# An adaLN attention and expert kernel: the scores of pairs at the clamped distance, from the content product instead of blocks of relative terms

## The chip, the cores and the metric

The kernel runs on one core of one Trainium2 chip. The metric is the device time of one execution in microseconds (us), lower is better. TensorE is called PE, VectorE DVE, ScalarE ACT, GpSimd POOL, and SP is the engine that here only issues DMAs.

## The reference, cut to what matters

There are 16 batches of 512 positions and 256 features, 16 heads of 16. After a layer norm with modulation comes an attention with relative position embeddings in both directions, then a second norm and a mixture of 8 experts of which the best two are summed. All is in float32. The part that the change touches:

```python
scores = jnp.einsum('bhqd,bhkd->bhqk', q, k)
dist_idx = pos_l - pos_r + M - 1                 # M = 256, S = 512
pos_emb = dist_emb[dist_idx]                     # dist_emb has 511 rows
rel_q = jnp.einsum('bhld,lrd->bhlr', q, pos_emb)
rel_k = jnp.einsum('bhrd,lrd->bhlr', k, pos_emb)
scores = (scores + rel_q + rel_k) / sqrt(D)
probs = softmax(scores)
```

The index runs up to 511 + 255, beyond the last row, 510. An index past the end is clamped to 510. For the last query tile (positions 384 to 511) and the first key tile (positions 0 to 127) every index is at least 512, so all pairs there have one and the same embedding row e. With q, k and e the score before the scale is then q.k + q.e + k.e = (q + e).(k + e) - e.e.

## The kernel before, in words

The work is cut into three kinds of pieces.

The **prologue** (`prepare`, one call per batch) normalizes a batch, transposes it on PE, forms q, k and v and stores them to DRAM. `normalize(b + 1)` is called inside `prepare(b)`, so DVE normalizes a batch while PE works on the one before. Between the calls for the first batches stands the setup: small loads, the gates, and the tables `t_f` and `t_r` (the embedding rows as PE's moving operand), loaded by 16 DMAs on SP at L509 and L512. `stationary` then rewrites q and k as stationary operands in DRAM.

A **block of terms** (class `Rel`, 64 of them) holds rel_q + rel_k for 128 pairs of batch and head, 64 queries and 128 keys. Block n stands for a half s of the batches, a query tile lb, a key tile rb and a half lh of the query tile. `q_set` (L165, four times per block) multiplies q with a table into four PSUM banks, which ACT copies out (L175). `k_set` (L186, four times) does it for k, and DVE adds the four banks (L195). `store` writes the block to `rel_d` in DRAM (L203). The first 10 blocks (`LEAD`) are made in the prologue, the rest beside the units.

A **unit** (64 of them) is one query tile of 128 positions of one batch, all 16 heads, from the scores to the output. Unit u has s = u // 32, lb = u % 32 // 8, so units 24 to 31 and 56 to 63 have the last query tile, lb = 3. For each of four groups of four heads: `load_scores` fetches the terms from `rel_d` into `st` (L582); `content` multiplies q with k, masked so that head pairs share a row group, four matmuls of 32 rows by 512 columns (L644), and DVE adds the terms and takes the row maxima (L650); ACT takes the exponentials (L660); `turn` transposes (L669) and ACT or DVE evicts; `context` multiplies with v (L687), and ACT copies the unit's context out once (`cT`, L695). After that: `project` with a norm (its `rstd`, a power, on POOL, L101), `residual` (three POOL operations, L754 to L756), `norm2` (stats on DVE, `rstd` on POOL again at L101, then `xn` on DVE, L768), `modulate` (transposes `fpt` of xn on PE, L778), `route`, and the experts in four pairs (L830), whose results DVE and ACT take from PSUM (L841, L845) and POOL sums up (L851 to L855). `mask_q` forms the masked q for the next unit with two POOL operations (`qm`, L614).

The order on every engine is written out by hand: each unit has 16 slots, and a step is put in a slot by `at(slot, order, function, ...)`. Steps of one slot run in the order of the second number. Each engine takes its instructions in that order. The lines that matter here, z being the unit's first slot:

```python
at(q0 - 12, 0, load_scores, u, g)   # q0 = z + 4 * g
at(q0 - 4, 5, content, u, g)
at(z - 13, 0, load_k, u, 0)
at(z - 6, 0, load_k, u, 1)
at(z - 7, 0, mask_q, u)
z += 16
at(z + 8, 0, residual, u)
at(z + 10, 0, norm2, u)
at(z + 11, 6, modulate, u)
n = u + LEAD                        # block n beside unit u
```

So `mask_q` of the next unit stands on POOL between `residual` and `norm2` of the unit before. PSUM has seven banks in one pool (`bank`), handed out in turn to all of these steps, and one for the context.

Of the kernel before, what the change touches and what calls it, by code (L numbers as in the profile page):

```python
# [8 lines left out]
F32 = mybir.dt.float32  # L9
U32 = mybir.dt.uint32  # L10
AF = mybir.ActivationFunctionType
ALU = mybir.AluOpType
AX = mybir.AxisListType
# [3 lines left out]
P = 128  # L17
E = 256
S = 512
H = 16  # L20
D = 16
# [5 lines left out]
NP = 64  # L27
HB = 8
LQ = 64
RK = 128  # L30
# [4 lines left out]
def adaln_attention_moe_kernel(  # L35
# [34 lines left out]
    nc = tc.nc  # L70
    NB = x.shape[0]
    NL = S // P
    NE = E // P
# [6 lines left out]
    const = ctx.enter_context(tc.tile_pool(name="const", bufs=1))  # L80
# [6 lines left out]
    par = const.tile([P, 2], F32, name="par")  # L87
# [5 lines left out]
    t_f = const.tile([P, 2, 2 * S], F32, name="t_f")  # L93
    t_r = const.tile([P, 2, 2 * S], F32, name="t_r")

    wo_sb = const.tile([P, NE, E], F32, name="wo_sb")
    gates_d = dram.tile([NB, 3, E], F32, name="gates_d")

# [16 lines left out]
    rel_d = [dram.tile([P, P, S], F32, tag=f"rel_{n}", name=f"rel_d{n}") for n in range(8)]  # L115
# [6 lines left out]
    def bank(name):  # L122
        return ps.tile([P, S], F32, tag="g", name=name)


    class Rel:


        def __init__(self):
            self.qe = {}  # L130
            self.ke = {}
            self.two = [rblk.tile([P, LQ, RK], F32, name=f"r_{i}") for i in range(2)]

        @staticmethod
        def at(n):
            s, m = n // 32, n % 32
            return s, m // 8, m % 8 // 2, m % 2

        def wants(self, n):

            s, lb, rb, lh = self.at(n)
            w = []
            if rb == 0:
                w += [("q", s, lb * 2 + lh, g) for g in range(2)]
            if lh == 0:
                w += [("k", s, rb * 2 + g // 2, g % 2) for g in range(4)]
            return w
# [60 lines left out]
    rel = Rel()  # L208


    with ExitStack() as pro:
# [205 lines left out]
        with tc.tile_pool(name="setup", bufs=1) as su:  # L417
# [7 lines left out]
            for name, w in (("wq", wq), ("wk", wk), ("wv", wv)):  # L425
                nc.scalar.dma_start(
                    out=w_sb[name], in_=w.rearrange("(kc p) n -> p kc n", p=P)
# [33 lines left out]
            for k, kind in enumerate((0, 1, 3, 4)):  # L461
                for cc in range(NE):
                    col = kind * E + cc * P
                    for kc in range(NE):
                        nc.tensor.matmul(
                            pm[:, k, cc, :], wm[:, kc, col : col + P], scT[:, kc, :],
                            start=(kc == 0), stop=(kc == NE - 1),
# [10 lines left out]
            for k, kind in enumerate((2, 5)):  # L478
                for kc in range(NE):
                    nc.tensor.matmul(  # L480
                        pg[:, k, :], scT[:, kc, :], wm[:, kc, kind * E : (kind + 1) * E],
                        start=(kc == 0), stop=(kc == NE - 1),
# [23 lines left out]
            for t in range(4):  # L506
                for i in range(2):
                    rows = slice(32 * t + 16 * i, 32 * t + 16 * i + 16)
                    nc.sync.dma_start(  # L509
                        out=t_f[rows, i, i : 2 * S], in_=ext[:, 0 : 2 * S - i]  # L510
                    )
                    nc.sync.dma_start(  # L512
                        out=t_r[rows, i, i : 2 * S - 1], in_=rev[:, 0 : 2 * S - 1 - i]
                    )
            m8 = su.tile([P, 8], F32, name="m8")
            nc.gpsimd.memset(m8, 1.0)
            nc.gpsimd.affine_select(
                out=m8, in_=m8, compare_op=ALU.is_ge, fill=0.0,
# [3 lines left out]
                out=m8, in_=m8, compare_op=ALU.is_ge, fill=0.0,  # L522
# [7 lines left out]
        for cc in range(NE):  # L530
            for pa in range(2):
                for t in range(4):
                    row = cc * P + t * 32 + pa * D
                    nc.sync.dma_start(
                        out=wo_sb[pa * 64 + t * D : pa * 64 + (t + 1) * D, cc, :],
                        in_=wo[row : row + D, :],
# [16 lines left out]
    u1 = ctx.enter_context(tc.tile_pool(name="u1", bufs=1))  # L553
    u2 = ctx.enter_context(tc.tile_pool(name="u2", bufs=2))
# [16 lines left out]
    def place(u):  # L571
        s, lb, bb = u // 32, u % 32 // 8, u % 8
        return s, lb, bb, s * HB + bb

    units = {}

    def load_scores(u, g):

        s, lb, bb, b = place(u)
        h0 = bb * H + (g // 2) * 8 + g % 2  # L580
        st = sp.tile([P, 4, S], F32, tag="s", name=f"s_{u}_{g}")
        nc.sync.dma_start(  # L582
            out=st, in_=rel_d[s * 4 + lb][h0 : h0 + 7 : 2].rearrange("h l r -> l h r")
        )
        units[u]["s", g] = st

    def load_k(u, cc):
        s, lb, bb, b = place(u)
        kt = kp.tile([P, S], F32, tag="k", name=f"k_{u}_{cc}")
        nc.sync.dma_start(  # L590
            out=kt,
            in_=k_d[s][bb * H + cc * 8 : bb * H + cc * 8 + 8].rearrange("h d l -> (h d) l"),
        )
        units[u]["k", cc] = kt

    def load_q(u):
        s, lb, bb, b = place(u)
        lcols = slice(lb * P, (lb + 1) * P)
        qs = u1.tile([P, NE, P], F32, tag="qs", name=f"qs_{u}")
        for cc in range(NE):  # L600
            nc.sync.dma_start(
                out=qs[:, cc, :],
                in_=q_d[s][bb * H + cc * 8 : bb * H + cc * 8 + 8, :, lcols].rearrange(
                    "h d l -> (h d) l"
                ),
            )
        units[u]["qs"] = qs

    def mask_q(u):

        qs = units[u].pop("qs")
        qm = u2.tile([P, 2, NE, P], F32, tag="qm", name=f"qm_{u}")
        for pa in range(2):
            nc.gpsimd.tensor_scalar(qm[:, pa], qs, par[:, pa : pa + 1], None, ALU.mult)  # L614
        units[u]["q"] = qm

    def load_rest(u):
        s, lb, bb, b = place(u)
# [18 lines left out]
    def content(u, g):  # L637

        t_ = units[u]
        cc, pa = g // 2, g % 2  # L640
        bs = [bank(f"qk_{u}_{g}_{t}") for t in range(4)]
        for t in range(4):
            rows = slice(32 * t, 32 * t + 32)
            nc.tensor.matmul(  # L644
                bs[t], t_["q"][rows, pa, cc, :], t_["k", cc][rows, :], start=True, stop=True
            )
        mx = u3.tile([P, 4], F32, tag="mx", name=f"mx_{u}_{g}")
        st = t_["s", g]
        for t in range(4):
            nc.vector.tensor_tensor_reduce(  # L650
                st[:, t, :], bs[t], st[:, t, :], 0.25, -3.0e38, ALU.add, ALU.max,
                mx[:, t : t + 1],
            )
        nc.vector.tensor_scalar(mx, mx, -1.0, None, ALU.mult)  # L654
        t_["m", g] = mx
# [180 lines left out]
    def expert_sums(u, pr):  # L836

        t_ = units[u]
        py = t_.pop("py")
        e = 2 * pr  # L840
        nc.vector.scalar_tensor_tensor(  # L841
            t_["y"], py[:, 0:E], t_["mask"][:, e : e + 1], t_["y"], ALU.mult, ALU.add
        )
        ye = u2.tile([P, E], F32, tag=f"ye{pr > 0}", name=f"ye_{u}_{pr}")
        nc.scalar.activation(  # L845
            ye, py[:, E : 2 * E], AF.Identity, scale=t_["mask"][:, e + 1 : e + 2]
        )
        if pr == 0:
            t_["y2"] = ye
        else:  # L850
            nc.gpsimd.tensor_tensor(t_["y2"], t_["y2"], ye, ALU.add)  # L851
        if pr == NX // 2 - 1:
            nc.gpsimd.tensor_tensor(t_["y"], t_["y"], t_["y2"], ALU.add)
            nc.gpsimd.tensor_tensor(t_["y"], t_["y"], t_["gf"], ALU.mult)
            nc.gpsimd.tensor_tensor(t_["y"], t_["y"], t_["x2"], ALU.add)  # L855
# [12 lines left out]
    for u in range(NP):  # L868
        z = 16 * u
        for g in range(4):  # L870
            q0 = z + 4 * g
            at(q0 - 12, 0, load_scores, u, g)
            at(q0 - 4, 5, content, u, g)
            at(q0 - 2, 7, exps, u, g, (0, 1))
            at(q0 - 1, 7, exps, u, g, (2, 3))
            for t in range(4):
                at(q0 + t, 3, turn, u, g, t, t > 0)
            at(q0 + 5, 4, context, u, g)
        at(z - 16, 0, lambda u: units.setdefault(u, {}), u)
        at(z - 13, 0, load_k, u, 0)  # L880
        at(z - 6, 0, load_k, u, 1)
        at(z - 15, 0, load_q, u)
        at(z - 7, 0, mask_q, u)
        at(z - 9, 0, load_rest, u)
        at(z + 15, 0, load_tail, u)
        z += 16
        at(z + 3, 6, back, u)
        at(z + 5, 3.5, contextT, u)
        at(z + 7, 6, project, u)
# [3 lines that stand above are left out]
        at(z + 13, 7, route, u)  # L893
        at(z + 15, 7, mask_t, u)
        at(z + 16, 7, bias, u)
        for pr in range(4):
            at(z + 18 + 4 * pr, 6, experts, u, pr)
            at(z + 19 + 4 * pr, 1, expert_sums, u, pr)
        at(z + 35, 0, finish, u)

        z -= 16
        n = u + LEAD
        if n < NP:
            for g in range(4):
                at(z + 1 + 4 * g, 6, rel.q_set, n, g)
                at(z + 15 + 4 * g, 2, rel.k_set, n, g)
            for g in range(4):
                at(z + 28 + 2 * g, 0, rel.store, n, g)
        if n + 1 < NP:
            for w in rel.wants(n + 1):  # L910
                o = 8 + w[3] if w[0] == "q" else (16, 17, 21, 25)[w[2] % 2 * 2 + w[3]]
                at(z + o, 0, rel.load, w)
# [52 lines left out]
```

## Time and profile before

| | |
|---|---|
| median of 3 runs | 2974.68 us (2971.85 to 2978.81) |
| profiled execution | 2971.56 us, span 2969.8 us |
| granted PE clock, mean of the span | 0.971 |
| busy share PE / DVE / ACT / POOL | 95% / 67% / 65% / 21% |
| first and last context copy (`cT`) | 528.8 us, 2934.5 us |
| L165 and L186, the blocks' matmuls, busy | 467.1 and 321.2 us |
| L644, content matmuls, busy | 388.9 us |
| moved by DMA | 796.46 MB |

Up to some 520 us lies the prologue with the first ten blocks, then the units follow each other. The first 54 have a block beside them, the last ten have none. Busy time of an engine is the union of its instructions. In a timeline each row has the start, the length, the engine, the line, the operation, what is written from what is read, the shape, how many instructions were merged into the row, and in brackets how long the engine stood idle before it and what it had waited for. "SPq" is the issue of a DMA, not its transfer.

### The profile page before, as it was taken

To read this page: it belongs to the slowest core of one execution; us is meant where nothing else is said; L and a number is where in the kernel's file an instruction comes from. 1 tells how busy PE (TensorE), PEld (TensorE's weight loads), DVE (VectorE), ACT (ScalarE), POOL (GpSimd) and SP (SyncE) were. 2 spreads that over 40 slices of the span, in tenths; PEclk is the share of its full clock that TensorE was granted. 3 is DMA by queue.
4 is the path that set the end of the run, shared out by engine and by line. 5 is a ranking of instruction groups with operands and counts; after the bars stand their busy time and mean duration, and the time that the engine had idled before them with its cause. 6 is when DMAs were issued, how large, how long until landed. Compare 5 with 4: busy or idle time off the path is not lost.

```text
span 2969.8 us, 75984 instructions
## 1 busy us (share of the span) xinstructions
PE 2815.0 (95%) x30186; PEld 1845.8 (62%) x30186; DVE 1984.0 (67%) x5396; ACT 1933.7 (65%) x3682; POOL 629.8 (21%) x863
## 2 busy tenths in 40 slices
PE   8889864999999999999999999999999999999997
PEld 5556552666666666666666666666666666666564
DVE  5446542777777777777767777677777767776664
ACT  2344433777776777777677677777767777767774
POOL 1000000121222222122222212222222222222333
PEclk9889866999999999999999999999999999999999
DMA  6879997798988889988888998888898888898661
GB/s 191 302 260 319 298 302 259 229 290 268 287 269 271 280 283 293 280 272 281 272 271 277 287 281 274 268 283 277 281 295 268 286 273 272 272 280 279 211 232 54
DMA packets 855346, 796.46 MB, mean 268 GB/s; under 512 B 25545, under 2 KB 649409, under 8 KB 854737
## 3 DMA queue, kind: packets, MB, share of 16 engines
q1 hardware_dynamic: 854032, 790.03, 84.3%
q8 instruction: 240, 3.93, 0.5%
q10 hardware_dynamic: 960, 1.57, 0.2%
q14 instruction: 114, 0.93, 0.1%
HBM read 462.20 MB, written 328.25 MB: 266 GB/s over the span
## 4 chain that ended last, share of the span: by engine, by line
PE 79%; POOL 2%; DMA 1%; DVE 1%; SPq 1%; issue 1%; ACT 1%; POOLq 0%; ACTq 0%; DVEq 0%
PE pt L669 18%; PE fpy L830 14%; PE pq L165 13%; PE qk L644 12%; PE pc L687 8%; PE pk L186 8%; PE ph L735 2%; PE fpl L791 1%; PE pcl L702 1%; POOL qm L614 1%; DMA vu<-v_d 1%; PE fpt L778 1%; PE fpb L821 0%; PE pct L719 0%; POOL rstd L101 0%
## 5 line engine op out<-in xcount | busy, mean ns | idle before, releaser
L175 ACT COPY r<-pq 128x512 f32<-128x512 f32 x1024 | 525.4, 603 | 385.8 <-PE pq L165 368.9
L195 DVE TENSOR_TENSOR r<-pk,r 128x512 f32<-128x512 f32 x1024 | 635.0, 683 | 192.8 <-PE pk L186 187.3
L660 ACT ACTIVATE s<-s,mx 128x512 f32<-128x512 f32 x1024 | 691.6, 735 | 50.2 <-DVE mx L654 47.2
L650 DVE CUSTOM_DVE_ANT_0 s<-qk,s 128x512 f32<-128x512 f32 x1024 | 644.0, 685 | 39.2 <-PE qk L644 36.7
L669 PE MATMUL pt<-ident,s 128*128 128x128 f32 x4096 | 652.0, 283 | 10.7 <-ACT s L660 10.3
L669 PEld LDWEIGHTS pt<-ident,s 128*128 128x128 f32 x4096 | 451.0, 142 | 289.3 <-issue 77.7
L672 ACT COPY pT<-pt 128x512 f32<-128x512 f32 x768 | 459.5, 598 | 252.1 <-PE pt L669 250.4
L851 POOL TENSOR_TENSOR ye<-ye,ye 128x256 f32<-128x256 f32 x192 | 140.6, 732 | 1633.0 <-ACT ye L845 1627.5
L830 PE MATMUL fpy<-we_sb,fhT 128*128 128x512 f32 x1024 | 483.4, 595 | 0.0
L165 PE MATMUL pq<-t_r,qe 32*128 32x256 f32 x4096 | 467.1, 417 | 4.0 <-DMA qe<-eq_d 2.9
L644 PE MATMUL qk<-k,qm 32*128 32x512 f32 x2048 | 388.9, 644 | 28.0 <-POOL qm L614 28.0
L186 PEld LDWEIGHTS pk<-t_f,ke 32*128 32x128 f32 x8192 | 268.8, 190 | 189.1 <-ACT pT L672 157.7
L841 DVE SCALAR_TENSOR_TENSOR fy<-fpy,fmask,fy 128x256 f32<-128x256 f32 x256 | 123.8, 483 | 384.6 <-PE fpy L830 375.6
L165 PEld LDWEIGHTS pq<-t_r,qe 32*128 32x128 f32 x4096 | 283.3, 186 | 143.1 <-DVE mx L650 67.8
L186 PE MATMUL pk<-t_f,ke 32*128 32x128 f32 x8192 | 321.2, 288 | 7.2 <-DVE r L195 3.4
L687 PE MATMUL pc<-pT,vu 128*32 128x128 f32 x8192 | 278.2, 277 | 0.0
L830 PEld LDWEIGHTS fpy<-we_sb,fhT 128*128 128x128 f32 x1024 | 175.4, 191 | 124.9 <-issue 124.9
L687 PEld LDWEIGHTS pc<-pT,vu 128*32 128x32 f32 x8192 | 209.2, 110 | 43.5 <-issue 42.9
L644 PEld LDWEIGHTS qk<-k,qm 32*128 32x128 f32 x2048 | 141.5, 183 | 104.6 <-DVE r L195 47.3
L674 DVE COPY pT<-pt 128x512 f32<-128x512 f32 x256 | 174.5, 682 | 24.9 <-PE pt L669 20.3
L101 POOL TENSOR_TENSOR rstd<-rstd,mhalf 128x1 f32<-128x1 f32 (+1 forms) x144 | 88.0, 611 | 438.5 <-DVE rstd L100 434.9
L845 ACT ACTIVATE ye<-fpy,fmask 128x256 f32<-128x256 f32 x256 | 127.5, 498 | 45.2 <-DVE fy L841 45.1
(111 smaller groups left out, 2175.6 us busy)
## 6 DMA issues: line engine op xcount, KB each, us to landing
rel_d<-r SPq DMA_DIRECT2D x256, 1024.0 KB, 8.5
s<-rel_d SPq DMA_DIRECT2D x256, 1024.0 KB, 7.8
vu<-v_d SPq DMA_DIRECT2D x64, 576.0 KB, 7.7
ke<-ek_d SPq DMA_DIRECT2D x128, 256.0 KB, 7.1
k<-k_d SPq DMA_DIRECT2D x128, 256.0 KB, 6.5
gt<-gates_d SPq DMA_DIRECT2D x64, 256.0 KB, 4.7
v_d<-v SPq DMA_DIRECT2D x16, 576.0 KB, 6.4
xt<-in_x SPq DMA_DIRECT2D x16, 512.0 KB, 6.1
```

Source lines behind the costliest of these rows:

```text
L165: nc.tensor.matmul(bs[t][:, a * 256 : (a + 1) * 256], e[32 * t : 32 * t + 32, (g % 2) * 2 + a, :], t_r[32 * t : 32 * t + 32, :, m0 : m0 + RK],
L175: nc.scalar.copy(dst[:, t], bs[t].rearrange("p (a c) -> p a c", a=2))
L186: nc.tensor.matmul(bs[t][:, a * 128 : (a + 1) * 128], e[32 * t : 32 * t + 32, a, :], t_f[32 * t : 32 * t + 32, :, m0 : m0 + LQ], start=Tru ...
L195: nc.vector.tensor_tensor(dst, bs[t].rearrange("p (r l) -> p l r", r=8), dst, ALU.add)
L644: nc.tensor.matmul(bs[t], t_["q"][rows, pa, cc, :], t_["k", cc][rows, :], start=True, stop=True)
L650: nc.vector.tensor_tensor_reduce(st[:, t, :], bs[t], st[:, t, :], 0.25, -3.0e38, ALU.add, ALU.max, mx[:, t : t + 1],)
L660: nc.scalar.activation(t_["s", g][:, t, :], t_["s", g][:, t, :], AF.Exp, bias=t_["m", g][:, t : t + 1])
L669: nc.tensor.transpose(pt[:, cols], t_["s", g][:, t, cols], ident)
L672: nc.scalar.copy(pT, pt)
L674: nc.vector.tensor_copy(pT, pt)
L687: nc.tensor.matmul(pc[32 * t : 32 * t + 32, g, :], t_["v"][:, rb, h * VW : h * VW + 32], pTs[t][:, rb * P : (rb + 1) * P], start=(rb == 0) ...
L830: nc.tensor.matmul(py, t_["hT"][:, kc, :], we_sb[:, kc, pr * 2 * E : (pr + 1) * 2 * E], start=(kc == 0), stop=(kc == NE - 1),)
```

## The change

The blocks of terms for the last query tile and the first key tile are left out: 4 of 64 (`todo` lists the 60 that remain). For the 16 units of that query tile, `load_scores` fetches the keys from 128 on, and POOL fills the first 128 columns with -e.e (`minus_ee`). `shift_k` adds e to the first 128 columns of k, in place, on POOL. `mask_q` forms beside q also `qf`, the masked q + e, with two more POOL operations. `content` cuts each matmul in two: 384 columns with q, and 128 columns with q + e. The embedding row comes in once, in the prologue: as a row on all partitions (`far_row`) and, with eight small DMAs, as a column repeated for eight heads (`far`); three DVE operations form -e.e. To make room in SBUF the first `ye` tile of a unit has one buffer instead of two.

The core of the diff:

```diff
+            self.todo = [n for n in range(64) if n % 32 // 2 != 12]
...
-            if rb == 0:
+            if rb == lb // 3:
                 w += [("q", s, lb * 2 + lh, g) for g in range(2)]
...
+            far_row = su.tile([P, D], F32, name="far_row")
+            last = dist_t[:, 510:511]
+                nc.sync.dma_start(
+                    out=far_row, in_=last.rearrange("d o -> (o d)").partition_broadcast(P)
+                )
+            for h in range(8):
+                nc.sync.dma_start(out=far[h * D : (h + 1) * D, :], in_=last)
+            nc.vector.tensor_tensor(far_row, far_row, far_row, ALU.mult)
+            nc.vector.tensor_reduce(
+                minus_ee, far_row.unsqueeze(1).to_broadcast([P, 4, D]), AX.X, ALU.add
+            )
+            nc.vector.tensor_scalar(minus_ee, minus_ee, -1.0, None, ALU.mult)
...
+        r0 = RK * (lb // 3)
         nc.sync.dma_start(
-            out=st, in_=rel_d[s * 4 + lb][h0 : h0 + 7 : 2].rearrange("h l r -> l h r")
+            out=st[:, :, r0:],
+            in_=rel_d[s * 4 + lb][h0 : h0 + 7 : 2, :, r0:].rearrange("h l r -> l h r"),
         )
+        if r0:
+            nc.gpsimd.tensor_copy(
+                st[:, :, 0:r0], minus_ee.unsqueeze(2).to_broadcast([P, 4, r0])
+            )
...
+    def shift_k(u, cc):
+        kt = units[u]["k", cc]
+        nc.gpsimd.tensor_scalar(kt[:, 0:RK], kt[:, 0:RK], far, None, ALU.add)
...
+        if place(u)[1] == 3:
+            qf = u1.tile([P, 2, NE, P], F32, tag="qf", name=f"qf_{u}")
+            for pa in range(2):
+                nc.gpsimd.tensor_scalar(
+                    qf[:, pa], qs, far, par[:, pa : pa + 1], ALU.add, ALU.mult
+                )
...
+            r0 = RK if "qf" in t_ else 0
             nc.tensor.matmul(
-                bs[t], t_["q"][rows, pa, cc, :], t_["k", cc][rows, :], start=True, stop=True
-            )
+                bs[t][:, r0:], t_["q"][rows, pa, cc, :], t_["k", cc][rows, r0:],
+                start=True, stop=True,
+            )
+            if r0:
+                nc.tensor.matmul(
+                    bs[t][:, 0:r0], t_["qf"][rows, pa, cc, :], t_["k", cc][rows, 0:r0],
+                    start=True, stop=True,
+                )
...
-        ye = u2.tile([P, E], F32, tag=f"ye{pr > 0}", name=f"ye_{u}_{pr}")
+        ye = (u2 if pr else u1).tile([P, E], F32, tag=f"ye{pr > 0}", name=f"ye_{u}_{pr}")
...
+        if u % 32 // 8 == 3:
+            at(z - 8, 0, shift_k, u, 0)
+            at(z - 2, 0, shift_k, u, 1)
...
-        if n < NP:
+        if n < len(rel.todo):
```

More of the change, by code (lines that the diff above doesn't have):

```diff
@@ L94, in adaln_attention_moe_kernel @@
     t_r = const.tile([P, 2, 2 * S], F32, name="t_r")
+    far = const.tile([P, 1], F32, name="far")
+    minus_ee = const.tile([P, 4], F32, name="minus_ee")
     wo_sb = const.tile([P, NE, E], F32, name="wo_sb")
@@ L131, in __init__, with at @@
             self.ke = {}
+            self.todo = [n for n in range(64) if n % 32 // 2 != 12]
             self.two = [rblk.tile([P, LQ, RK], F32, name=f"r_{i}") for i in range(2)]
-        @staticmethod
-        def at(n):
-            s, m = n // 32, n % 32
+        def at(self, n):
+            s, m = self.todo[n] // 32, self.todo[n] % 32
             return s, m // 8, m % 8 // 2, m % 2
@@ L514, in adaln_attention_moe_kernel @@
                     )
+            far_row = su.tile([P, D], F32, name="far_row")
+            last = dist_t[:, 510:511]
+            with nc.allow_non_contiguous_dma(reason="one column of the table"):
+                nc.sync.dma_start(
[8 more added lines that the diff above has]
+            nc.vector.tensor_scalar(minus_ee, minus_ee, -1.0, None, ALU.mult)
             m8 = su.tile([P, 8], F32, name="m8")
@@ L615, in mask_q @@
         units[u]["q"] = qm
+        if place(u)[1] == 3:
[4 more added lines that the diff above has]
+                )
+            units[u]["qf"] = qf
     def load_rest(u):
@@ L908, in adaln_attention_moe_kernel @@
                 at(z + 28 + 2 * g, 0, rel.store, n, g)
-        if n + 1 < NP:
+        if n + 1 < len(rel.todo):
             for w in rel.wants(n + 1):
```

## The prediction

> **What bounds the kernel now.** I read the page first: TensorE (PE) is busy 95% of the span, no other compute engine above 67%.
> ```profile
> PE 2815.0 (95%) x30186; PEld 1845.8 (62%) x30186; DVE 1984.0 (67%) x5396; ACT 1933.7 (65%) x3682; POOL 629.8 (21%) x863
> ```
> Then the timeline of ScalarE: the copy cT (L695) comes once per unit, so the distance between two is the unit's period. The first pair is a unit with a block of terms beside it, the second one of the last units, which have none.
> ```profile
> 2004.46 0.59 ACT L695 COPY cT<-pc 128x512 f32<-128x512 f32 x1 [0.40 <-PE pc L687]
> 2044.51 0.59 ACT L695 COPY cT<-pc 128x512 f32<-128x512 f32 x1 [0.40 <-PE pc L687]
> ...
> 2793.93 0.59 ACT L695 COPY cT<-pc 128x512 f32<-128x512 f32 x1 [0.40 <-PE pc L687]
> 2822.43 0.59 ACT L695 COPY cT<-pc 128x512 f32<-128x512 f32 x1 [0.40 <-PE pc L687]
> ```
> The periods are 40.05 and 28.50 us: a block costs 11.55 us of its unit. The windows of one period each say what bounds it (after the length: busy us of PE, weight loads, DVE, ACT, POOL).
> ```profile
> 2010.00:2050.05 40.05, 40.05 (x460) 26.21 (x459) 28.65 (x78) 28.60 (x56) 9.49 (x13) 1.00 0.95 300
> 2782.00:2810.50 28.50, 26.64 (x265) 17.30 (x265) 19.18 (x62) 20.58 (x40) 9.49 (x14) 1.00 0.62 220
> ```
> With a block PE is never idle; without one it idles 1.86 us. The timelines show where. First, a unit with a block:
> ```profile
> 2025.83 0.73 POOL L756 TENSOR_TENSOR x<-x,xu 128x256 f32<-128x256 f32 x1
> 2026.53 1.83 POOL L614 TENSOR_SCALAR qm<-qs,par 128x256 f32<-128x256 f32 x2
> 2028.33 0.57 POOL L101 TENSOR_TENSOR rstd<-rstd,mhalf 128x1 f32<-128x1 f32 x1
> ...
> 2027.95 0.15 DVE L100 TENSOR_SCALAR rstd<-mv 128x1 f32<-128x1 f32 x1
> 2028.94 0.41 DVE L768 TENSOR_SCALAR xn<-x,mv,rstd 128x256 f32<-128x256 f32 x1 [0.83 <-POOL rstd L101]
> 2030.55 1.29 DVE L195 TENSOR_TENSOR r<-pk,r 128x512 f32<-128x512 f32 x2 [0.60 <-PE pk L186]
> ...
> 2030.95 0.38 PE L778 MATMUL fpt<-ident,xn 128*128 128x128 f32 x2
> ```
> rstd's input is ready at 2028.10, but GpSimd takes it at 2028.33, as qm ends: it works in program order and has no room left here. DVE waits for rstd before xn; behind xn stand the evictions L195, whose banks the next content matmuls need. PE's transposes of xn have 1.6 us of room. In a tail unit they have none:
> ```profile
> 2810.86 0.57 POOL L101 TENSOR_TENSOR rstd<-rstd,mhalf 128x1 f32<-128x1 f32 x1
> ...
> 2811.47 0.41 DVE L768 TENSOR_SCALAR xn<-x,mv,rstd 128x256 f32<-128x256 f32 x1 [0.85 <-POOL rstd L101]
> ...
> 2811.93 0.44 PE L778 MATMUL fpt<-ident,xn 128*128 128x128 f32 x2 [1.86 <-DVE xn L768]
> ```
> So the chain rstd, xn, fpt ends last in the tail. The third place is the prologue, where SP issues the tables and DVE normalizes batch 3:
> ```profile
> 52.59 0.64 SPq L512 DMA_DIRECT2D t_r<-rev  x1
> ...
> 42.52 0.42 DVE L251 BATCH_NORM_STATS2 stats<-xt 128x6 f32<-128x256 f32 x1
> 46.08 1.38 DVE L256 TENSOR_SCALAR xt<-xt,mv,rstd 128x256 f32<-128x256 f32 x4 [1.13 <-POOL rstd L101]
> ...
> 53.80 1.04 PE L269 MATMUL hTp<-ident,xt 128*128 128x128 f32 x8
> ```
> DVE is done at 47.46, PE wants the batch at 53.80: 6.3 us of room.
>
> **What the Trainium skill says.** "GPSIMD Engine Reference", section 3.1: 512 elements of a one-input loop took 769 ns; two-input ones run at about 2.6 cycles an element. The trace agrees roughly: L756, 256 elements, takes 0.73. "TensorE: Matmul & The Clock Gate", Part 3, "What overlaps and what doesn't": matmuls start in strict order, and weight loads pass running matmuls only in other row groups. The trace differs: of the content matmuls (four row groups, two passes each) the first passes of all four start within 0.02 us, and the second of the first group only 0.53 us later. The same page, "Why this matters for your kernels": idle gaps over about 3 us halve the clock. The trace agrees: PE idles 114.3 to 124.9, and the window after it has clock 0.51.
> ```profile
> 125.00:131.00 6.00, 6.00 (x17) 3.81 (x18) 2.97 (x11) 1.86 (x3) 0.00 (x0) 0.51 0.68 190
> ```
> "DMA: Bandwidth & Descriptors", "Rules for kernel authors": a last dimension that isn't contiguous becomes one descriptor per element.
>
> **The change part by part**, against the profiled execution (2971.56 us: span 2969.8 and 1.8 around it; 3.1 under the median of the runs, 2974.68).
>
> *Blocks.* 60 of 64 stay, so units 50 to 53 have none: 4 x 11.55 = **-46.2**. Their 64 ACT and 64 DVE evictions, 16 stores and 8 loads (and the fourth of each score load in 16 units) lie beside PE and are in the period or worth nothing. The blocks after the left-out ones run two or four units earlier in the same slots, from tables that the prologue wrote: nothing.
>
> *Content matmuls.* In 16 units (query tile 3) each of 16 is cut in 384 + 128 columns: 64 groups of four. Columns stay equal. L186 puts 16 matmuls of 128 columns in 1.17 us, L644 four of 512 in 1.14: +0.01 to 0.1 a group if the row groups go on side by side; I take 0.06: **+4** (bounds 0 and 9; the serial case is a rival).
>
> *GpSimd.* Each of the 16 units gets four copies of -e.e (128x4x128), two shifts of k (128x128) and two instructions for qf (128x256, two operations). In the order of the built program, one copy, one shift and both qf stand between L756 and norm2's rstd. The others fall where GpSimd idles (9 and 16 us before its L851) and cost nothing, unless that cover goes. Prices: qf like qm, 0.92 at least, 1.2 at most, taken 1.0; shift, half of qm, 0.45 to 0.6, taken 0.55; the copy between L223/L501's memset rate (1.06 for 1152, 1.81 for 2048: 0.53 for 512) and qm's rate (1.76), taken 0.8 by the skill's 769 ns. Delay of rstd: 0.8 + 0.55 + 2.0 = 3.35 us (2.8 to 4.8).
> - Units 24 to 31, prepared beside blocks: xn 3.35 later; DVE's own idle up to L195 (0.12 + 0.60) absorbs 0.72; L195 frees its banks 2.63 later, and PE, waiting for fpt and then for those banks, is 2.63 late. PE has no idle to make it up: 8 x 2.63 = **+21.0**.
> - Units 56 to 63, in the tail: all of it, 8 x 3.35 = **+26.8**. PE then idles 5.2 us a unit, past the 3 us: about half of these gaps bring a half-speed stretch of 3.4 us, 1.7 lost: **+7** (0 to 14).
>
> The copies wait for the transposes of the buffer's last user, which PE passes 6 us before GpSimd comes; the shift waits for k, issued 2016.38, landing in 6.5, 4 us before its turn. One buffer less for the first ye: its reader L853 ends over 4 us before the next write. Nothing.
>
> *Prologue.* Nine DMAs stand on SP behind t_r, so far_row issues near 53.3. It moves 2048 single elements. DVE multiplies far_row right after batch 1's v, ahead of batch 3's normalization: it stands from 42.5 until it lands. Nearest rows: t_r 3.3 us to landing, bcol (256 single elements, in traffic) 7.5; bounds 56.6 and 64, I take 60. Then 0.7 us of new DVE work and 4.94 (42.52 to 47.46): PE starts at 65.7 instead of 53.8, **+12** (8.6 to 16), and some 3 us at half clock after the gap, as after 124.9: **+3**. Nothing later gives it back: from 93 us SP waits for PE.
>
> Sum: -46.2 + 4 + 21.0 + 26.8 + 7 + 15 = **+27.6**. On the median: 2974.7 + 27.6 = **3002**. Bounds of the same case: -46.2 + 17 + 22.7 + 8.6 = +2; and -46.2 + 9 + 32.6 + 38.4 + 14 + 19 = +67.
>
> **The rivals.**
> - *GpSimd's additions are short and the saving wins (faster).* Place: the same queue between L756 and rstd. At the memset's rate they are 0.53 + 0.21 + 0.62 = 1.36 us: 8 x 0.64 + 8 x 1.36 = 16, with 8.6 of prologue -21.6: 2953. It decides below a delay of some 2.1 us. For it: the skill's one-input rate. Against it: qm itself, 0.93 for 256 elements. 13%.
> - *The cut matmuls line up.* If a row group takes no second matmul until its first has begun its last pass, the next group starts 0.4 to 0.7 later, three times: +1.2 to 2.1 us for each of 64 groups, +77 to +134 on top: some 3105. For it: the skill's strict order. Against it: second passes already wait without stopping other groups. 15%.
> - *It cancels*: the low bounds meet, +2, 2977. 10%.
> - *The forecast*: 62%.
>
> That the change doesn't do what it says is excluded: the built program has 60 blocks.
>
> **How the numbers follow.** A measurement tells about 0.2% (6 us) from no change. Faster by more: 0.13, the first rival. Within: 0.10. Slower: 0.77, the forecast and the lining up. The range runs from 2974, the low bound, to 3050, past the high bound of the forecast; outside stay the faster rival and most of the lining up.
>
> **What would show it.** Units 24 to 31 prepared with periods of 42.7, the last eight of 32 to 33, four more units of 28.5; POOL's rstd behind qf; PE's idle before fpt above 4 us; DVE waiting for far_row until about 60. The sum is wrong if fpt shows no longer wait, if PE meets 53.8, or if the group of L684 takes over 2 us.

## The result, and the profile after

| | before | after |
|---|---|---|
| median of 12 runs each | 2975.22 us (2971.28 to 2979.26) | 2982.70 us (2976.79 to 2988.99) |
| ratio | | 1.0022, 95% interval 1.0012 to 1.0033 |
| profiled execution | 2971.56 us | 2987.41 us, span 2985.7 |
| first and last context copy | 528.8, 2934.5 us | 540.1, 2946.9 us |
| moved by DMA | 796.46 MB | 760.78 MB |

The changed kernel is slower by 7.5 us; 27.6 were forecast. The profiled pair lies further apart than the medians, 15.9 us, since the profiled run after is 4.7 us above its median and the one before 3.7 below. Both kernels were therefore profiled again, side by side (below).

The first part of the page after: PE has 256 matmul records fewer and is idle for more of a longer span, POOL has 128 instructions more.
```profile
PE 2788.7 (93%) x29930; PEld 1852.1 (62%) x29930; DVE 1948.3 (65%) x5335; ACT 1900.7 (64%) x3618; POOL 701.2 (23%) x991
```
The timeline of ScalarE, two pairs of context copies: units 24 to 31 are prepared in periods of 41.38 us (before 40.05), and the eight periods in which units 56 to 63 are prepared (below: the last eight) take 32.3 to 33.6 us (before 28.50).
```profile
1415.07 0.59 ACT L736 COPY cT<-pc 128x512 f32<-128x512 f32 x1 [0.40 <-PE pc L728]
1456.45 0.58 ACT L736 COPY cT<-pc 128x512 f32<-128x512 f32 x1 [0.40 <-PE pc L728]
...
2754.63 0.58 ACT L736 COPY cT<-pc 128x512 f32<-128x512 f32 x1 [0.40 <-PE pc L728]
2787.72 0.58 ACT L736 COPY cT<-pc 128x512 f32<-128x512 f32 x1 [0.40 <-PE pc L728]
```
The windows of one such period each (length, then busy us of PE, weight loads, DVE, ACT, POOL, then PE's clock). In the first, PE idles 1 us where it never idled, and the rest of the added 1.33 us lies inside its recorded busy time; in the second it idles 4.1 us and runs at a mean clock of 0.91.
```profile
1441.00:1482.40 41.40, 40.41 (x497) 28.17 (x489) 28.57 (x77) 28.57 (x56) 14.03 (x22) 1.00 0.82 254
2746.00:2779.00 33.00, 28.86 (x305) 20.50 (x301) 19.95 (x62) 20.69 (x39) 14.01 (x21) 0.91 0.46 158
```
The timeline of POOL around norm2's `rstd` in a unit prepared beside a block:
```profile
1477.83 0.73 POOL L797 TENSOR_TENSOR x<-x,xu 128x256 f32<-128x256 f32 x1
1478.50 0.61 POOL L605 COPY s<-minus_ee 128x512 f32<-128x512 f32 x1
1479.09 0.62 POOL L620 TENSOR_SCALAR k<-k,far 128x128 f32<-128x128 f32 x1
1479.68 1.83 POOL L640 TENSOR_SCALAR qm<-qs,par 128x256 f32<-128x256 f32 x2
...
1481.49 1.09 POOL L646 TENSOR_SCALAR qf<-qs,far,par 128x256 f32<-128x256 f32 x2
1482.55 0.57 POOL L104 TENSOR_TENSOR rstd<-rstd,mhalf 128x1 f32<-128x1 f32 x1
1483.16 0.41 DVE L809 TENSOR_SCALAR xn<-x,mv,rstd 128x256 f32<-128x256 f32 x1 [2.94 <-POOL rstd L104]
```
Copy, shift and `qf` stand where the prediction put them. From start to start they take 0.59, 0.59 and 1.06 us, 2.24 in all (3.35 forecast), and DVE waits 2.94 us for `rstd` where it waited 0.83. PE then waits for `xn`, and once more, by the trace, for a bank that ScalarE's `ye` frees; `ye` itself waits for DVE's `fy`, which stands behind `xn`:
```profile
1483.72 0.41 PE L819 MATMUL fpt<-ident,xn 128*128 128x128 f32 x2 [0.59 <-DVE xn L809]
1484.62 0.63 PE L710 MATMUL pt<-ident,s 128*128 128x128 f32 x4 [0.49 <-ACT ye L886]
...
1484.00 0.47 ACT L886 ACTIVATE ye<-fpy,fmask 128x256 f32<-128x256 f32 x1 [1.48 <-DVE fy L882]
```
In a tail unit the same wait ends at PE, which stood 1.86 us there before:
```profile
2773.80 0.57 POOL L104 TENSOR_TENSOR rstd<-rstd,mhalf 128x1 f32<-128x1 f32 x1
2774.41 0.41 DVE L809 TENSOR_SCALAR xn<-x,mv,rstd 128x256 f32<-128x256 f32 x1 [2.94 <-POOL rstd L104]
...
2774.96 0.66 PE L819 MATMUL fpt<-ident,xn 128*128 128x128 f32 x2 [4.13 <-DVE xn L809]
```
The groups of the added instructions (busy us, mean ns of one). One `qf` takes 550 ns with its two operations, one `qm` of the same shape 926 ns with one operation.
```profile
L640 POOL TENSOR_SCALAR qm<-qs,par 128x256 f32<-128x256 f32 x128 | 117.0, 926 | 144.8 <-DMA k<-k_d 131.7 <-DMA qs<-q_d 13.1
L605 POOL COPY s<-minus_ee 128x512 f32<-128x512 f32 x64 | 39.0, 610 | 66.4 <-ACT ye L886 43.2 <-ACT s L701 13.9 <-PE pt L710 9.3
L620 POOL TENSOR_SCALAR k<-k,far 128x128 f32<-128x128 f32 x32 | 19.6, 611 | 0.0
L646 POOL TENSOR_SCALAR qf<-qs,far,par 128x256 f32<-128x256 f32 x32 | 17.4, 550 | 0.0
```
And the prologue: `far_row` is issued at 53.57 and has landed at 60.12, DVE stands idle 17.29 us until then, and PE starts batch 3 at 64.79 instead of 53.80.
```profile
53.57 0.63 SPq L522 DMA_DIRECT2D far_row<-in_dist_t  x1
54.25 6.18 SPq L526 DMA_DIRECT2D far<-in_dist_t  x8
60.12 0.17 DVE L527 TENSOR_TENSOR far_row<-far_row 128x16 f32<-128x16 f32 x1 [17.29 <-DMA far_row<-in_dist_t]
...
64.79 2.25 PE L273 MATMUL hTp<-ident,xt 128*128 128x128 f32 x8 [10.53 <-issue]
```

### The profile page after: what moved, and what is told of

It is laid out like the page before. It is cut to its first block, busy times and chain, and to the rows that moved or that the text cites. A ratio compares the mean times of both kernels' runs of the same rounds, so it can differ in the third digit from the quotient of the medians.

```text
span 2985.7 us, 75461 instructions
## 1 busy us (share of the span) xinstructions
PE 2788.7 (93%) x29930; PEld 1852.1 (62%) x29930; DVE 1948.3 (65%) x5335; ACT 1900.7 (64%) x3618; POOL 701.2 (23%) x991
## 2 busy tenths in 40 slices
DMA packets 823487, 760.78 MB, mean 255 GB/s; under 512 B 27480, under 2 KB 651344, under 8 KB 822880
## 4 chain that ended last, share of the span: by engine, by line
PE 83%; POOL 5%; DMA 3%; DVE 3%; issue 3%; ACT 2%; SPq 0%; ACTq 0%; POOLq 0%; DVEq 0%
PE pt L710 16%; PE fpy L871 13%; PE pq L169 13%; PE qk L679 11%; PE pk L190 8%; PE pc L728 8%; PE wqp L299 2%; PE vp L317 2%; PE wkp L299 2%; POOL qm L640 1%; PE ph L776 1%; PE fpl L832 1%; DVE r L199 1%; PE pcl L743 1%; POOL rstd L104 1%
## 5 line engine op out<-in xcount | busy, mean ns | idle before, releaser
L179 ACT COPY r<-pq 128x512 f32<-128x512 f32 x960 | 492.5, 605 | 361.1 <-PE pq L169 344.4
L199 DVE TENSOR_TENSOR r<-pk,r 128x512 f32<-128x512 f32 x960 | 595.2, 683 | 183.9 <-PE pk L190 176.7
L691 DVE CUSTOM_DVE_ANT_0 s<-qk,s 128x512 f32<-128x512 f32 x1024 | 644.0, 685 | 47.3 <-PE qk L679 32.3
L710 PEld LDWEIGHTS pt<-ident,s 128*128 128x128 f32 x4096 | 457.4, 143 | 270.9 <-issue 89.8
L169 PE MATMUL pq<-t_r,qe 32*128 32x256 f32 x3840 | 437.0, 419 | 4.2 <-DMA qe<-eq_d 2.9
L679 PE MATMUL qk<-k,qm 32*128 32x512 f32 (+1 forms) x2048 | 376.1, 634 | 24.6 <-POOL qm L640 24.6
L190 PEld LDWEIGHTS pk<-t_f,ke 32*128 32x128 f32 x7680 | 252.6, 190 | 176.4 <-ACT pT L713 145.6
L169 PEld LDWEIGHTS pq<-t_r,qe 32*128 32x128 f32 x3840 | 265.4, 186 | 133.8 <-DVE mx L691 62.7
L190 PE MATMUL pk<-t_f,ke 32*128 32x128 f32 x7680 | 301.8, 287 | 6.8 <-DVE r L199 3.1
```

Of the source, the lines that this page charges most:

```text
L169: nc.tensor.matmul(bs[t][:, a * 256 : (a + 1) * 256], e[32 * t : 32 * t + 32, (g % 2) * 2 + a, :], t_r[32 * t : 32 * t + 32, :, m0 : m0 + RK],
L179: nc.scalar.copy(dst[:, t], bs[t].rearrange("p (a c) -> p a c", a=2))
L190: nc.tensor.matmul(bs[t][:, a * 128 : (a + 1) * 128], e[32 * t : 32 * t + 32, a, :], t_f[32 * t : 32 * t + 32, :, m0 : m0 + LQ], start=Tru ...
L199: nc.vector.tensor_tensor(dst, bs[t].rearrange("p (r l) -> p l r", r=8), dst, ALU.add)
L679: nc.tensor.matmul(bs[t][:, r0:], t_["q"][rows, pa, cc, :], t_["k", cc][rows, r0:], start=True, stop=True,)
L691: nc.vector.tensor_tensor_reduce(st[:, t, :], bs[t], st[:, t, :], 0.25, -3.0e38, ALU.add, ALU.max, mx[:, t : t + 1],)
```

## The experiments

The theory after these traces: the four blocks save 46 us; GpSimd's additions ahead of `rstd` take most of it back in 16 units, partly through PE's clock; the DMAs of the embedding row take some 11 us in the prologue. Every kernel below was timed beside the kernel before, and ratios are to those runs, with 95% intervals.

**1. The embedding row loaded early** (e1_far_early): the nine DMAs moved up behind the loads of the table.
```diff
             nc.sync.dma_start(out=rev[:, 767:1023], in_=dist_rt[:, 0:256])
+            far_row = su.tile([P, D], F32, name="far_row")
+            ...                                # the nine DMAs of far_row and far
...
-            far_row = su.tile([P, D], F32, name="far_row")
-            ...
```


> Against the changed kernel. Theory (the nine far DMAs stand behind the table loads on SP, land at 60.1 us, DVE waits for them in front of batch 3's normalization, PE therefore starts batch 3 at 64.8 instead of 53.8): with the nine DMAs issued early in the setup the wait is gone, PE starts batch 3 near 53.8, the first context copy comes at 529 instead of 540.1, the time falls by 11 us. Rival (SP is full in the setup, nine DMAs of some 0.7 us each push the other setup loads back by 6 us wherever they stand, or the new DVE operations themselves hold batch 3): PE still idles 6 to 11 us somewhere before 70 us, the first context copy stays at 535 or later, the time falls by less than 5 us. Units: periods as in the changed kernel (41.4 beside blocks, 33.1 in the last eight).

Measured: 2968.3 us, ratio 0.9966 (0.9952 to 0.9979). PE starts batch 3 at 53.98, the periods of the units are unchanged. So the delay was DVE's wait for the row, and the rival falls: issued at 14 us, the nine DMAs push nothing that is needed. But the first context copy comes at 521.6, 18.6 us earlier than after and 7 us earlier than in the kernel before, which no theory expected. Something in the change makes the prologue *faster*; experiments 5, 11 and 12 look for it.

**2. GpSimd's queue ahead of norm2's rstd cleared** (e2_pool_clear): no instruction less, four kinds of them elsewhere, in units of the last query tile.
```diff
+            if u % 32 // 8 == 3:
+                at(q0 - (9 if g == 1 else 12), 0, fill, u, g)
...
-        at(z - 13, 0, load_k, u, 0)
+        at(z - (15 if u % 32 // 8 == 3 else 13), 0, load_k, u, 0)
...
-            at(z - 8, 0, shift_k, u, 0)
+            at(z - 10, 0, shift_k, u, 0)
...
-        at(z - 7, 0, mask_q, u)
+        at(z - (10 if u % 32 // 8 == 3 else 7), 0, mask_q, u)
+        at(z - 6, 0, mask_qf, u)
```
`fill` makes the copies of -e.e, which stood in `load_scores`; `mask_qf` forms `qf` alone, now behind `rstd`.

> Against the changed kernel. The four kinds of additions on GpSimd (copy, shift, qf, and qm of these units) are moved out of the way of norm2's rstd; no instruction less. Theory (the whole loss in the units is rstd taken late by GpSimd in 16 units): the periods of units 24 to 31's preparation fall from 41.38 to 40.05 (8 x 1.33 = 10.6 us), those of the last eight from 33.07 to 28.5 (8 x 4.57 = 36.6 us), half-clock windows in the tail vanish, the time falls by 47 us; the prologue keeps its 11 us. Rival (a part of the longer periods comes from the content matmuls cut in 384 and 128 columns, or from the score loads): periods stay above 28.5 in the tail by 1 us or more, the time falls by less than 38 us.

Measured: 2948.12 us, ratio 0.9895 (0.9879 to 0.9910), some 36 us under the changed kernel. Beside blocks the periods are back at 40.08: that part of the theory holds. In the last eight they are 28.62 in two units and 30.1 to 30.2 in six. The time is the rival's, but not its reason: a unit of 28.62 has cut content matmuls too.

**3. Both moves** (e3_both): the edits of 1 and 2 together.

> Both moves together. Theory: 11 + 47 us less than the changed kernel, and 46 us less than the kernel before, that is only the four blocks' 4 x 11.55 remain: 2925 to 2930. Rival (the two losses share a cause, or the freed time is lost again to a later wait): less than 45 us under the changed kernel.

Measured: 2932.29 us, ratio 0.9840 (0.9827 to 0.9854), a few us short of the forecast, with the first context copy at 522.6 and again six of the last eight periods at 30.1 to 30.2. Windows of two neighbouring tail units in this kernel:
```profile
2764.00:2792.60 28.60, 26.63 (x297) 18.95 (x297) 19.46 (x62) 20.63 (x39) 14.06 (x22) 1.00 0.52 181
2792.60:2822.80 30.20, 28.19 (x297) 19.89 (x297) 19.49 (x63) 20.75 (x39) 14.07 (x22) 0.94 0.55 175
```
Same instructions, same idle time of PE (2.0 us); the second is longer by PE's own busy time, 1.56 us, at a clock of 0.94: one stretch of 3.4 us at half speed. What stands ahead of the idle time is `qf`, now behind `rstd` and so beside `xn`, which takes 0.66 us instead of 0.41 (timeline of a tail unit):
```profile
2822.11 1.12 POOL L650 TENSOR_SCALAR qf<-qs,far,par 128x256 f32<-128x256 f32 x2
2822.15 0.66 DVE L813 TENSOR_SCALAR xn<-x,mv,rstd 128x256 f32<-128x256 f32 x1 [0.66 <-POOL rstd L104]
...
2822.95 0.41 PE L823 MATMUL fpt<-ident,xn 128*128 128x128 f32 x2 [2.00 <-DVE xn L813]
```

**4. Only copy and shift away** (e4_copy_shift_away): the edits of 2 without those on `mask_q`, so that `qf` alone delays `rstd`.

> Only the copy and the shift that stand ahead of norm2's rstd are moved away, the two qf operations (1.09 us) stay; rstd's delay falls from 2.27 to some 1.06 us. Theory (delay plus a clock step: PE's idle gap of 4.1 us in the tail brings half clock, one of 2.9 us doesn't): tail periods 29.6 (8 x 3.5 = 28 us less), no half-clock window in the tail, units beside blocks 40.05 to 40.4 (8 us less), together 36 us under the changed kernel. Rival (no step: what is beyond the delay goes with it in proportion, 4.57/2.27 per us): tail periods 28.5 + 2.1 = 30.6 with half-clock windows in about half of the units, 28 us less in all. Rival 2 (the clock isn't part of it, the extra 2.3 us a unit come from the cut content matmuls): tail periods 31.9, 18 us less in all.

Measured: 2967.44 us, ratio 0.9957 (0.9943 to 0.9970), some 16 us under the changed kernel. Beside blocks 40.51. In the tail 31.4 to 32.7, mean 31.90: the number of the second rival, but every one of the eight units has a half-clock stretch of 3.4 or 6.8 us. PE's gap is 3.25 us, not 2.9, since here too `xn` is slowed, by the next copy in the queue:
```profile
2758.91 0.61 POOL L607 COPY s<-minus_ee 128x512 f32<-128x512 f32 x1
2758.99 0.67 DVE L810 TENSOR_SCALAR xn<-x,mv,rstd 128x256 f32<-128x256 f32 x1 [1.91 <-POOL rstd L104]
...
2759.81 0.66 PE L820 MATMUL fpt<-ident,xn 128*128 128x128 f32 x2 [3.25 <-DVE xn L810]
```
A step of the clock between 2.9 and 4.1 us, as the theory had it, is not there: all eight gaps of 3.25 us bring a stretch, and in experiments 2 and 3 six of eight gaps of 2.0 us do.

**5 and 6. Both kernels again, side by side on one chip** (e5_before_again, e6_after_again; no edit). Kernels 7 and 8 ran there too.

> The kernel before, unchanged, on this chip. First context copy at 528.8 us and PE's wait in front of the first content matmul 28.0 us, if the trace of before is typical; or some 4 to 7 us earlier with a wait of 24.5 us as in every trace of a changed kernel so far, if that part of the prologue only scatters. Units as before (40.05 and 28.50 us).

> The changed kernel, unchanged, on this chip, to compare the others with. If the profiled execution (2987.4 us, 4.7 above the median) is typical in its parts: first context copy at 540.1, last eight units 33.07 us each on average, 15.9 us above the kernel before in the trace; if the medians (+7.5 us) are right, half of the surplus is missing in the prologue or in the number of half-clock stretches of the tail.

Measured: before 2976.65 us, after 2983.69 us; ratios 0.9997 (0.9988 to 1.0007) and 1.0018 (1.0009 to 1.0026). The spans of the two traces, 2973.0 and 2979.3, differ by 6.3 us, about as the medians do, and serve for the sum below. The first context copies come at 529.1 and 539.1, and PE's wait before the first content matmul is 28.2 and 24.5 us, as in the first pair: this difference of the wait isn't scatter. What does scatter is the tail of before: three of its last units have a stretch at half clock (30.05 us) in this trace, one in the first.

**7. qf ahead of norm2 again** (e7_room), in the place that `qm` left free:
```diff
-        at(z - 6, 0, mask_qf, u)
+        at(z - 7, 0, mask_qf, u)
```


> Against the version with both moves (2932.3 us). The only edit: qf's two operations stand ahead of norm2 again (between the residual's last operation and norm2's rstd, where GpSimd was idle for 1.6 us once qm had gone), instead of behind rstd. Theory (qf running beside xn lengthens xn from 0.41 to 0.66 us, PE's gap grows from 1.85 to 2.0 us, and at 2.0 us six of eight units get a half-clock stretch of 3.4 us, which costs 1.6 us): xn 0.41, gap 1.85, tail periods 28.5, 11 us less: 2921. Rival (half-clock stretches in the tail come from PE's lower load by the last query tile as such, not from the gap): periods alternate between 28.6 and 30.2 as before, within 2 us of 2932.

Measured: 2937.55 us, ratio 0.9873 (0.9858 to 0.9888): no gain. `qf` no longer runs beside `xn`, but the copy behind `rstd` moved up and does:
```profile
2796.47 0.61 POOL L607 COPY s<-minus_ee 128x512 f32<-128x512 f32 x1
2796.55 0.67 DVE L813 TENSOR_SCALAR xn<-x,mv,rstd 128x256 f32<-128x256 f32 x1 [0.67 <-POOL rstd L104]
```
So the gap stays at 2.0 to 2.3 us, with six of eight periods at 30.18 or more. The trial didn't reach the gap that it was to test.

**8. All blocks computed** (e8_all_blocks).
```diff
-            self.todo = [n for n in range(64) if n % 32 // 2 != 12]
+            self.todo = list(range(64))
...
-            if rb == lb // 3:
+            if rb == 0:
```


> The changed kernel, but all 64 blocks of terms are computed and stored again; the four for the clamped distance aren't read. Theory (a block costs its unit 40.05 - 28.50 = 11.55 us of PE): four units more of 40.05 and four fewer of 28.5, 46 us above the changed kernel, some 3030. Rival (PE's time for the four blocks was hidden, and what the change lost is all in other places): less than 20 us above the changed kernel.

Measured: 3031.01 us, ratio 1.0179 (1.0165 to 1.0193): 47.3 us above the changed kernel. The saving of the blocks is there in full, and the rival falls.

**9. The copy for group 1 one slot later as well** (e9_room2).
```diff
-                at(q0 - (9 if g == 1 else 12), 0, fill, u, g)
+                at(q0 - (8 if g == 1 else 12), 0, fill, u, g)
```


> Against the last version (qf ahead of norm2, 2937.6 us). There it wasn't qf that ran beside xn, but the next GpSimd operation in the queue, the copy of -e.e for group 1, and xn took 0.67 us again. Edit: this copy one slot later, behind the expert sum. Theory (xn is slowed from 0.41 to 0.67 us by any GpSimd operation beside it; with 1.85 us PE's gap brings a half-clock stretch in fewer than half of the units, with 2.0 us and more in three of four): xn 0.41, gap 1.85, tail periods 28.5 with at most three of 30.1, 8 to 15 us less than 2937.6. Rival (the tail's half-clock stretches follow from the load of these units as such): gap 1.85, but periods of 30.1 in six of eight units, within 4 us of 2937.6.

Measured: 2923.43 us, ratio 0.9812 (0.9799 to 0.9825). A tail unit:
```profile
2788.48 0.55 POOL L104 TENSOR_TENSOR rstd<-rstd,mhalf 128x1 f32<-128x1 f32 x1 [0.54 <-DVE rstd L103]
2789.07 0.41 DVE L813 TENSOR_SCALAR xn<-x,mv,rstd 128x256 f32<-128x256 f32 x1 [0.67 <-POOL rstd L104]
...
2789.62 0.41 PE L823 MATMUL fpt<-ident,xn 128*128 128x128 f32 x2 [1.77 <-DVE xn L813]
```
Nothing on POOL beside `xn`, 0.41 us, gap 1.77, and the last six periods are 28.38 to 28.39 each, without a half-clock stretch; of the seven units with this gap only the first has one. The rival, that these units' load as such brings the half clock, falls. The length of the gap doesn't decide alone, though. Counted over the units without a block in all fourteen traces, a stretch of the half clock comes with 1 of 7 gaps of 1.76 to 1.77 us, 13 of 56 of 1.82 to 1.86, 16 of 21 of 1.94 to 2.02, 6 of 12 of 2.25 to 2.78, and all 56 above 3.1.

This version beats both kernels, by 1.9% the one before. The first `ye` tile has its single buffer here too, so with periods of 40.08 and 28.39 us that part of the change costs next to nothing.

**10. Content matmuls uncut** (e10_uncut): this kernel leaves out q.e for the pairs at the clamped distance.
```diff
-            r0 = RK if "qf" in t_ else 0
+            r0 = 0
```


> The changed kernel with the content matmuls uncut: q alone on all 512 columns, qf is formed but not used, so q.e is missing in the pairs at the clamped distance. Theory (cut matmuls cost nothing, as the groups' 1.10 and 1.08 us say): periods 41.38 and 33.07 as in the changed kernel, time within 4 us of 2983.7. Rival (the cut costs 0.06 us or more a group or keeps PE from making up time): 4 to 20 us less.

Measured: 2981.67 us, ratio 1.0011 (1.0002 to 1.0020), not to be told from the 1.0018 of the changed kernel. Periods 41.37 beside blocks; the last eight 262.7 us together against 263.9. By the periods the cut costs some 1 us in all; the two ratios leave room for a few us.

**11 and 12. The addresses of r.** The changed kernel allocates `far` and `minus_ee` (64 bytes of each partition as allocated) ahead of `wo_sb`; all later tiles move by as much. `r`, the source of the blocks' stores, starts at byte 36032 of a partition before and at 36096 after. Experiment 11 puts an unused tile of 64 bytes into the kernel before, experiment 12 allocates the two new tiles behind `r` and the blocks' stationary tiles (`stp`; the expectation calls them score tiles), so that only `wo_sb`, `r` and `stp` are back at their old addresses.
```diff
 # 11, in the kernel before
+    pad = const.tile([P, 16], F32, name="pad")
+    nc.gpsimd.memset(pad, 0.0)
     wo_sb = const.tile([P, NE, E], F32, name="wo_sb")
 # 12, in the changed kernel
-    far = const.tile([P, 1], F32, name="far")
-    minus_ee = const.tile([P, 4], F32, name="minus_ee")
...
     stp = ctx.enter_context(tc.tile_pool(name="stp", bufs=5))
+    const2 = ctx.enter_context(tc.tile_pool(name="const2", bufs=1))
+    far = const2.tile([P, 1], F32, name="far")
+    minus_ee = const2.tile([P, 4], F32, name="minus_ee")
```


> The kernel before with one unused tile of 64 bytes per partition in front of wo_sb, so that r and the tiles behind it lie at SBUF addresses that are multiples of 128, as they do in the changed kernel (there through far and minus_ee), instead of 64 beyond one. Theory (stores of r run at 348 instead of 290 GB/s from there, and the prologue's later part, where SP's queue is full, gains by it): the DMA rate beside the stores 348, PE's wait before the first content matmul 24.5 instead of 28.2, first context copy at 521 to 525 instead of 529, the time 4 to 8 us under the kernel before. Rival (the faster prologue comes from elsewhere in the change, such as the order of the loads): 290 GB/s, 528.8, no difference.

> The changed kernel with far and minus_ee allocated behind r and the score tiles, so that r lies again 64 beyond a multiple of 128 as in the kernel before; the same instructions. Theory of the addresses: stores of r at 290 GB/s, PE's wait before the first content matmul 28.2, first context copy at 543 to 547 instead of 539.5, the time 4 to 8 us above the changed kernel. Rival: as the changed kernel, 348 GB/s, no difference.

Measured: 11: 2970.52 us, ratio 0.9970 (0.9960 to 0.9981), first context copy at 523.6. 12: 2992.97 us, ratio 1.0040 (1.0026 to 1.0054), first context copy at 545.3. Both go the way of the theory of the addresses; 11 gains 9 us (6 to 12) where 4 to 8 were expected. The last stores of the prologue and what waits behind them on SP, first in the kernel before (experiment 5), then with the pad (11), then in 12:
```profile
460.78 9.64 SPq L203 DMA_DIRECT2D rel_d<-r  x4
470.83 3.29 SPq L558 DMA_DIRECT2D we_sb<-in_we_t  x1
486.48 2.09 PE L644 MATMUL qk<-k,qm 32*128 32x512 f32 x8 [28.23 <-POOL qm L614]
```
```profile
456.89 8.18 SPq L205 DMA_DIRECT2D rel_d<-r  x4
465.47 2.37 SPq L560 DMA_DIRECT2D we_sb<-in_we_t  x1
479.01 2.09 PE L646 MATMUL qk<-k,qm 32*128 32x512 f32 x8 [24.65 <-POOL qm L616]
```
```profile
474.89 9.63 SPq L208 DMA_DIRECT2D rel_d<-r  x4
484.62 3.59 SPq L576 DMA_DIRECT2D we_sb<-in_we_t  x1
500.02 2.09 PE L680 MATMUL qk<-k,qm 32*128 32x512 f32 x8 [27.66 <-POOL qm L641]
```
And the DMA rate in 40 slices of 448 to 486 us, experiment 5, then 11: while the stores run (the long even stretch), some 285 GB/s against 348. The other traces agree: over the 10 us that begin 1.5 us after the issue of these stores the rate is 282 in the three with `r` at 36032 and 348 in the eleven with 36096, and PE's wait before the first content matmul is 27.7 to 28.2 us in the three, 24.3 to 24.7 in the eleven.
```profile
GB/s 412 205 261 306 166 112 0 0 0 0 274 278 0 0 147 289 289 266 286 291 280 272 289 290 271 283 287 294 292 181 271 414 388 414 423 399 124 313 379 407
```
```profile
GB/s 190 84 0 0 0 0 315 237 0 0 201 348 349 346 348 348 347 348 349 346 348 348 264 425 427 405 388 414 294 139 370 410 418 417 404 385 386 386 379 397
```
The Trainium skill has a reason for it: "DMA: Bandwidth & Descriptors", section "How a descriptor splits into AXI transactions", says that a descriptor that doesn't start on a multiple of 256 bytes begins with a transaction that is fetched from the boundary below. A block's row in `r` is 512 bytes; 36032 is 192 above a multiple of 256, 36096 is one. By its rule such a row costs 8 + 8 + 6 = 22 beats of 32 bytes instead of 16, which gives an estimate of 0.73 for the rate; the traces show 285/348 = 0.82. The direction agrees, the size is less. That the effect comes with the shift of these tiles is shown, from both sides, and in the slow stretch nothing but 512-byte rows and a few 4-byte packets moves; that the split is its mechanism is the page's word and wasn't tried.

## Why the prediction was right or wrong

Right was the side (slower), the three places, and that PE's room decides what each costs. The size was wrong, first of all in the step that priced `qf`. The sum again, with the two traces of experiments 5 and 6:

| term | forecast, us | measured, us | from |
|---|---|---|---|
| four blocks less | -46.2 | -45.7 | the four periods; 8 gives 47.3 |
| content matmuls cut | +4 | 0 | 10 |
| units 24 to 31 | +21.0 | +10.7 | the eight periods, 41.38 against 40.05 each |
| tail, `rstd` later | +26.8 | +18.3 | 8 x (4.13 - 1.84) of PE's gap |
| tail, clock | +7 | +13.1 | the rest of 263.9 - 232.6 us of the last eight |
| prologue | +15 | +16.1 | first context copy, 12 against 5 |
| tiles moved by 64 bytes | not seen | -6.2 | first context copy, 6 against 12 |
| sum | +27.6 | +6.3 | the spans |

The two terms from the first context copy rest on single traces. In six traces with the prologue of the changed kernel (after, 2, 4, 6, 8, 10) it comes between 535.0 and 540.6, so each is sure to some 3 us only; the shorter wait of PE before the first content matmul shows 3 to 4 us of the 6.2 in every trace.

- **qf was mis-sized.** The step "qf like qm, 0.92 at least": the trace has 0.55 for one, with two operations instead of one. The copy (0.59 against 0.8) and the shift (0.59 against 0.55) were near. The delay of `rstd` was 2.24 us instead of 3.35, and below the lower bound of 2.8. This is the largest miss, 18.8 of the 21.3 us by which the sum is off: with it the units beside blocks lose 1.33 each instead of 2.63, and the tail 2.29 instead of 3.35. The room of 0.72 us was near (2.11 later at `xn`, 1.33 at PE), though by the trace the bank that PE waits for is one that `ye` frees and not one of the blocks' evictions. The faster rival was placed at a delay below 2.1: the case lay just beside it.
- **The half clock was under-sized.** The step "about half of these gaps bring a half-speed stretch" fell: all eight do, in five or six of them over 6.8 us. The threshold of 3 us, taken from the Trainium skill's "TensorE: Matmul & The Clock Gate", "Why this matters for your kernels", doesn't hold here: 16 of 21 gaps of some 2.0 us and 13 of 56 of some 1.84 us had a stretch (the count at 9). The kernel before had such stretches itself, which cost it 4.7 us in experiment 5 and which the prediction took for none (its 28.50 was a period without one).
- **The prologue was right** in size and mechanism (experiments 1 and 12). "Nothing later gives it back" was right as to slack and yet failed: 6.2 us came from the addresses, a side effect of two small tiles that the prediction didn't look at. Timed, it is 9 us (6 to 12) in experiment 11, and 6.5 between the ratios of 12 and 6.
- **The cut matmuls** cost next to nothing, and the rival that they line up is refuted: a group that nothing holds up takes 1.10 us to the next matmul (1.07 before), as the forecast expected against the page's strict order.
- **The cancelling case** came nearest in time, but not by its reason: the low bounds didn't meet. GpSimd's delay fell below its own, the prologue lay near the middle of its range, and a saving that was in no list came on top.
- **The right side was partly luck.** The surplus is 6 to 7.5 us, and two errors of that size cancel in it: the clock took 6.1 us more than forecast, and the addresses gave back 6.2 that nobody had foreseen.

## What to carry to other kernels

Work moved to an engine with 80% idle time is free only where its queue has room: find the instruction behind it that somebody waits for, and place the new ones behind that instead (here 45 us between versions 1 and 9, which do the same work). Price an operation by a row of its own form; the number of operations in it was no guide. And when two builds differ by a shift of tiles, read the DMA rate of the same stores in both before giving the difference to the edit.

## What the runs showed of the hardware

- Stores of 512-byte rows from SBUF ran at 282 to 285 GB/s from addresses 192 bytes above a multiple of 256, and at 348 from a multiple. Other offsets weren't tried.
- PE's clock fell to half for 3.4 us around idle gaps of some 2.0 us in units that are otherwise busy, in 16 of 21 cases; a stretch cost 1.6 us. With gaps of some 1.84 us it was 13 of 56, with gaps above 3.1 us all 56.
- `xn` on DVE (128x256) takes 0.41 us alone and 0.66 to 0.67 beside a GpSimd operation (`qf`, the copy) that has just begun. The Trainium skill's "SBUF — State Buffer", "Who interferes with whom", says that the two engines share a pair of ports, and that in some of its modes DVE is blocked until a GpSimd instruction that came first has ended. The rows fit: in experiment 7 `xn` ends 0.14 us after the copy. That `xn` runs in such a mode is not shown.
- On GpSimd a TENSOR_SCALAR of 128x256 took 926 ns with one operation and 550 with two. Why was not tried.
